# Layer 2 around a selective scan: the last sample's closing stage, halo affines, strip copies and a depthwise half rearranged

## The chip, the cores and the metric

The kernel runs on one core of one Trainium2 chip. The metric is the device time of the whole program in microseconds (us), the median of several runs.

## The reference, cut to what matters

The input is four samples of 128 channels by 128 x 128 pixels in float32. Four layers are applied to each sample, each as `x = x + layer(group_norm(x))`: a deformable convolution (layer 0), a dilated convolution in three factors (layer 1), a two-branch block with a selective scan (layer 2) and a convolution with an edge term (layer 3). The change lies in layer 2:

```python
x = cf_layernorm(x, pre_w, pre_b)          # over channels
x1, x2 = jnp.split(x, 2, axis=1)           # two halves of 64 channels
x1 = dwconv(x1, dw_w)                      # 3x3 depthwise
# ss2d(x2): in_proj -> (xx, z); xx = silu(dwconv(xx, conv_w) + conv_b)
#   forward_core: 4 directions (rows, columns, both reversed), 16 states:
#     h = h * exp(delta * A) + (delta * u) * B;   y = sum_n h * C  (+ D * u)
#   y = out_norm_w * normalised(y) + out_norm_b
#   y = y * silu(z);   out = y @ out_proj_w.T
y = interleave(x1, x2)                     # channel by channel
return cf_layernorm(y, post_w, post_b)
```

## The kernel before, in words

**Tiling.** A sample is 32 blocks of four rows, 512 pixels each (`NBLK`, `R`, `N`), with the 128 channels on the partitions. Intermediate images lie in DRAM.

**The scan.** `scan` is the main thread: 4 samples x 4 directions x 32 blocks = 512 blocks. A block has 128 channels times 16 states, held as four groups `g` of 128 x 4 x 512. For each group DVE multiplies `delta * u` (in PSUM, `dub`) with `bb` (L948) and then runs four scan instructions (L994), each of which needs a decay `pa`, an exponential made by ACT (L877, called by `decays`). One (g, ng) pair is a slot; a block has 16 slots. The outputs `h * cb` are taken on POOL (L917), summed over states on PE (L891), and copied out by `finish` (L901), which runs in slot 6 of the next block and queues the store of `y`. `prepare` makes `delta` two blocks ahead, a step per slot, on PE (`pdt` L810, `pxbc` L826), ACT (L815 to L832) and POOL (L836 to L842).

**Work beside the scan.** All other stages are generators that yield the fraction that they have done. `together` issues a slot of the scan and then pulls from the side chain `while at < f`, so the side keeps pace with the scan; `around(b)` says which stages lie beside the scan of sample b, with a weight each, and `chain` turns weights into fractions. Within a stage `weave` runs a pipeline: in round t it walks through the groups of `order`, and a step `(k, what)` handles block t-k; `MORE` advances a step that is itself a generator. There is a yield after each group. The program order on every engine is the order of issue, kept by hand (`keep_order`). Stores go through `store`, which issues them on SP a given number of ticks later; there is one tick per slot.

**layer2_pre** (L602 to L766) has 25 groups a round. It centres and normalises a block (`centre`, `square`, `spread_variance`, `invert`, `scale`), applies the affine while it writes the windows a and b of six rows (`affine`: six ACT instructions in one go, two for the block's rows and two each for the halo rows of its neighbours, L685), copies shifted rows into the windows' other halves by DMA (`shift`), and then convolves (`convolve`): six products of 128 channels for the scan's branch (`px`, L708) and six products of 64 for the depthwise half (`py`, L710), two passes each. `copy`, `gate` and `finish_strip` take the results out; every second block, `finish_strip` runs two Silus on ACT between two table loads (L740 to L742) and then, on ACT, copies the strip in column order into `cols` (L750).

**layer2_post** (L1010 to L1156) has 16 groups a round and 42 rounds. It adds up the directions (`centre`), normalises, multiplies with the gate, projects by three products (`ow_w` with the normalised y times gate, `ow_b` with the gate alone, `evc` with the depthwise half), normalises again (`square_out`, L1107 on the last two samples copies `pj` out of PSUM) and adds the skip. `measure` queues the store to `x3d`. Round n may start only when `ready(n)`: in the last direction block n-2 has been summed.

**The last sample.** Beside its scan run `layer2_post` and `layer3` of sample 2, their weights 16 and 22 times 2.5, and then its own `layer2_post` with weight 33, so that this begins 95 blocks into the 128 of the sample. What is left of it when the scan ends, and the last `layer3`, run alone.

```python
for f in main(pull):
    while at < f and pull():
        pass
    tick()
```

Of the kernel before, what the change touches and what calls it, by code (L numbers as in the profile page):

```python
# [18 lines left out]
P = 128  # L19
H = 128  # L20
# [16 lines left out]
THETA = 0.7  # L37
TW = W + 1
# [72 lines left out]
def conv_preact_kernel(ctx: ExitStack, tc: tile.TileContext, a: dict, nb: int):  # L111
# [120 lines left out]
    def image(name, parts=P):  # L232
        return dram.tile([parts, HW], F32, name=name)
# [368 lines left out]
    def layer2_pre(st):  # L602
        CH = 32
        x2d, stats = st["x2"], st["stats2"]
        zd, yd = image("zd"), image("yd", HALF)
# [3 lines left out]
        with ExitStack() as s:  # L609
# [11 lines left out]
            diag = wp.tile([P, 6, HALF], F32, name="diag")  # L621
            for t in range(6):
                nc.vector.tensor_mul(convw[:, t, :], convw[:, t, :], inx)
                nc.vector.tensor_scalar_mul(diag[:, t, :], eye2, dww[:, t : t + 1])
                yield 0.0
            sc, sh = gn_affine(stats)
# [48 lines left out]
            def affine(i):  # L675

                d = got.pop(("d", i)).rearrange("p (r w) -> p r w", w=W)
                jobs = [(i, slice(1, R + 1), slice(0, R))]
                if i > 0:
                    jobs.append((i - 1, slice(R + 1, R + 2), slice(0, 1)))  # L680
                if i + 1 < NBLK:
                    jobs.append((i + 1, slice(0, 1), slice(R - 1, R)))
                for m, to, of in jobs:
                    for t, part in zip(window(m), (slice(HALF, P), low)):
                        nc.scalar.activation(  # L685
                            t[part, to, :], d[part, of, :], AF.Identity,
                            bias=vec[part, V_PREB : V_PREB + 1], scale=vec[part, V_PREW : V_PREW + 1],
                        )

# [5 lines left out]
            def convolve(i):  # L695
                a, b = got["w", i]
                if not (stored(a) and stored(b)):
                    flush()
                got["u", i] = px = bank(0, "px")
                got["y", i] = py = bank(1, "py")  # L700
                px3 = px.rearrange("p (r w) -> p r w", w=W)
                py3 = py[low].rearrange("p (r w) -> p r w", w=W)
                use = [(1, 0, 0), (0, 0, -1), (2, 0, 1), (4, 1, 0), (3, 1, -1), (5, 1, 1)]
                for n, (t, ty, tx) in enumerate(use):
                    first, final = n == 0, n == len(use) - 1
                    co, cf = span(tx, W)
                    rf = slice(1 + ty, 1 + ty + R)
                    nc.tensor.matmul(px3[:, :, co], convw[:, t, :], a[:, rf, cf], start=first, stop=final)  # L708
                    yield
                    nc.tensor.matmul(py3[:, :, co], diag[:, t, :], b[:, rf, cf], start=first, stop=final)  # L710
                    yield

            def copy(i):
                j, q = divmod(i, BPB)
# [15 lines left out]
            def finish_strip(i):  # L730
# [8 lines left out]
                yield  # L739
                nc.scalar.activation(u, u, AF.Silu)  # L740
# [9 lines left out]
                nc.scalar.copy(got["c"][:, :, o : o + SB].rearrange("p w h -> p h w"), u)  # L750
                if (y0 + SB) % CH == 0:
                    c0 = y0 + SB - CH
                    for q in range(4):
# [8 lines left out]
                     [MORE], [(4, affine), (5, shift)], [MORE], [MORE], [(3, scale)], [MORE], [],  # L762
                     [(6, copy)], [(6, gate)], [], [(6, finish_strip), MORE], [MORE], [MORE]]
# [5 lines left out]
    def scan(pull):  # L769
# [240 lines left out]
    def layer2_post(st, engine=nc.gpsimd):  # L1010
# [6 lines left out]
        with ExitStack() as s:  # L1017
# [4 lines left out]
            event = load(wp, a["event"], [P, HALF], "event_sb")  # L1022
# [5 lines left out]
            ow_w = wp.tile([P, P], F32, name="ow_w")  # L1028
            nc.vector.tensor_scalar_mul(ow_w, po[:, 0:P], col(V_ONW))
            ow_b = wp.tile([P, P], F32, name="ow_b")  # L1030
            nc.vector.tensor_scalar_mul(ow_b, po[:, 0:P], col(V_ONB))
            pe = bank(1, "pe0")
            nc.tensor.matmul(pe[0:HALF, 0:P], event, cmat, start=True, stop=True)
            evc = wp.tile([HALF, P], F32, name="evc")
            nc.scalar.copy(evc, pe[0:HALF, 0:P])
# [19 lines left out]
            def fetch_gate(i):  # L1055
                got["z", i] = load(lp, blk(st["z"], i), [P, N], "zl", bufs=5)
                got["y", i] = load(lp, blk(st["y1"], i), [HALF, N], "yl", bufs=5)
# [33 lines left out]

            def gated(i):
                d = got["d", i]
                nc.gpsimd.tensor_mul(d, d, got["z", i])
# [45 lines left out]
            def ready(n):  # L1140
                return st["summed"] > min(max(n - 2, -1), NBLK - 1) and stored(st["y"])

            order = [[(2, r(fetch)), (3, r(fetch_gate)), (7, r(fetch_skip))], [(4, r(centre))],
                     [(5, r(spread_variance))], [(9, r(affine))], [(0, fetch_columns), (10, r(measure))],
                     [(4, r(square)), (5, r(invert))], [], [(7, r(spread_out))], [(9, r(add))], [(6, r(project))],
                     [(7, r(invert_out))], [(5, r(whiten)), (5, r(gated))], [(8, r(scale))], [], [(6, r(square_out))], []]
            if engine is nc.vector:
# [4 lines left out]
                         [(4, r(whiten))], [(5, r(square_out))], [(4, r(gated))], [(5, r(spread_out))], [],  # L1152
                         [(5, r(invert_out))]]
# [107 lines left out]
    def together(main, side):  # L1261

        at = 0.0

        def pull():
            nonlocal at
            f = next(side, 1.0)
            at = at if f is None else f
            return f is not None

        for f in main(pull):
            while at < f and pull():
                pass
            tick()
        drain(side)
# [4 lines left out]
    def loads(engine, stage, spare=False):  # L1280
# [3 lines left out]
        beside.clear()  # L1284
# [19 lines left out]
    def around(b):  # L1304
# [11 lines left out]
def layouts(i):  # L1316
# [54 lines left out]
    x["event"] = c((np.repeat(np.eye(HALF, dtype=f), 2, axis=1) * (np.arange(P) % 2 == 0).astype(f)).T)  # L1371
# [25 lines left out]
```

## Time and profile before

| what | us |
|---|---|
| median of three runs | 22394.33 (22386.31 to 22396.27) |
| profiled execution, its own time | 22863.03 |
| its span | 22861.3 |
| before the scan | 0 to 2552 |
| the scan | 2552 to 22532 |
| `layer2_pre` (samples 0 to 3) | 2291 to 3280, 6379 to 7766, 11873 to 13074, 17171 to 18372 |
| `layer2_post` (samples 0 to 3) | 7766 to 8331, 13074 to 13639, 18372 to 19596, 21249 to 22587 |
| `layer3` of the last sample, alone | 22587 to 22861 |

The profile is one execution with every instruction recorded; it is 2.1% longer than the median of the runs. In its lines a group reads: source line, engine, operation, output <- inputs, shapes, count, then busy time and mean ns of one, then the engine's idle time just before such instructions and what ended most of that. PE is TensorE, PEld its weight loads, DVE VectorE, ACT ScalarE, POOL GpSimd, SP the queue that issues DMAs. A table of stretches has the stretch, its length, then busy time with (x instructions) for each engine, or for the chosen line alone, and last the granted TensorE clock, the share of time that the DMA engines were busy, and GB/s. A line of waits has engine, line, what it waited for, and the total in us, the number of times and the longest. A timeline line has start, duration, engine, line, operation, tiles and in brackets the idle time before it with what ended that.

### The profile page before, as it was taken

What the parts mean: (1) busy time and instruction counts of PE and PEld (TensorE: products, weight loads), DVE (VectorE), ACT (ScalarE), POOL (GpSimd) and SP (SyncE); (2) the same over time, 40 slices, a digit from 0 to 9 for tenths busy, and PEclk for the clock granted to TensorE, in tenths of its full rate; (3) what the DMA queues carried; (4) which work ended last, traced back from release to release, by engine and by line L of the source; (5) the groups of instructions that cost most, each with busy time, mean ns of one, the idle gap of its engine ahead of it and who ended that gap; (6) DMA issues with size and microseconds to landing.
All of it is one profiled execution on the core that took longest, in us unless ns stands there. A gap on an engine that the chain in (4) does not pass through costs nothing. (4 is left out here: it accounts for less than half of the span.)

```text
span 22861.3 us, 179349 instructions
## 1 busy us (share of the span) xinstructions
PE 16937.6 (74%) x38024; PEld 6604.5 (29%) x38024; DVE 18834.7 (82%) x19765; ACT 16444.8 (72%) x37282; POOL 17193.3 (75%) x11496
## 2 busy tenths in 40 slices
PE   3445886666878888766689888766688978778768
PEld 1112222222323333222233333322232323233223
DVE  3443489999998899888898899988898899999863
ACT  4665677888778766788868776688877867666553
POOL 3554477787788888777788788877778889877763
PEclk7667898888989999887799999977899999999989
DMA  7556468777756777777776687777776677555653
GB/s 216 176 173 186 149 204 289 246 244 238 249 202 211 220 237 258 240 245 235 239 246 206 208 252 243 248 239 243 245 254 203 209 222 220 190 195 201 195 171 112
DMA packets 2560083, 5005.34 MB, mean 219 GB/s; under 512 B 1059136, under 2 KB 1330952, under 8 KB 2416656
## 3 DMA queue, kind: packets, MB, share of 16 engines
q1 hardware_dynamic: 2190352, 3785.61, 51.1%
q0 software_dynamic: 368640, 1208.25, 17.5%
q8 instruction: 310, 5.08, 0.1%
q14 instruction: 781, 6.40, 0.1%
HBM read 4065.12 MB, written 857.74 MB: 215 GB/s over the span
## 5 line engine op out<-in xcount | busy, mean ns | idle before, releaser
L994 DVE TENSOR_TENSOR_SCAN h<-pa,carry,h 128x512 f32<-128x512 f32 x8192 | 9999.6, 1268 | 977.3 <-ACT pa L877 764.5
L917 POOL TENSOR_TENSOR h<-h,cb 128x1024 f32<-128x1024 f32 x3740 | 8779.6, 2360 | 1429.8 <-ACT carry L911 1416.5
L891 PE MATMUL yacc<-h,gather_sb 128*128 128x512 f32 x15264 | 8345.2, 676 | 1600.5 <-POOL h L917 1106.9
L421 POOL DMA_INDIRECT g<-table,idx x4608 | 4542.8, 986 | 2073.0 <-issue 1273.7
L877 ACT ACTIVATE pa<-spread,neg_a 128x512 f32<-128x512 f32 x8192 | 5482.6, 682 | 279.2 <-DVE h L994 232.4
L948 DVE TENSOR_TENSOR h<-dub,bb 128x2048 f32<-128x2048 f32 x2048 | 4664.7, 2278 | 626.2 <-ACT dub L857 386.5
L891 PEld LDWEIGHTS yacc<-h,gather_sb 128*128 128x128 f32 x15264 | 3117.0, 216 | 5970.8 <-issue 3375.1
L458 PE MATMUL pst<-ident,v 128*128 128x128 f32 x4608 | 1190.9, 371 | 3038.5 <-DVE v L450 1719.6
L911 ACT COPY carry<-h 128x2 f32<-128x2 f32 x4096 | 769.4, 188 | 3089.9 <-DVE h L994 3084.6
L435 ACT ACTIVATE g<-g,wt 128x128 f32<-128x128 f32 x9216 | 2851.9, 389 | 113.6 <-DMA g<-table,idx 64.3
L447 DVE TENSOR_TENSOR pw<-pw,g 128x512 f32<-128x512 f32 x2304 | 1599.2, 694 | 1439.1 <-ACT pw L435 1180.3
L435 ACT ACTIVATE pw<-g,wt 128x128 f32<-128x128 f32 x4608 | 1695.6, 368 | 760.4 <-remote 278.2
L458 PEld LDWEIGHTS pst<-ident,v 128*128 128x128 f32 x4608 | 718.5, 159 | 4394.0 <-issue 2406.8
L836 POOL TENSOR_TENSOR e<-e,one_e 128x512 f32<-128x512 f32 x512 | 650.2, 1270 | 1372.0 <-ACT one_e L830 1304.3
L468 PE MATMUL acc<-smp,w_sb 128*128 128x512 f32 x2304 | 1558.3, 765 | 77.3 <-DVE x L475 68.9
L857 ACT COPY dub<-spread 128x512 f32<-128x512 f32 x2048 | 1199.3, 586 | 421.4 <-DVE h L948 241.9
L450 DVE SCALAR_TENSOR_TENSOR v<-g,wt,pw 128x128 f32<-128x128 f32 x4608 | 1293.3, 343 | 114.0 <-DVE pw L447 1.8
L1212 PE MATMUL p<-xn,w_l_sb 128*128 128x508 f32 (+2 forms) x2304 | 1138.6, 612 | 1.8 <-ACT xn L1191 1.8
L708 PE MATMUL px<-win,convw_sb 128*128 128x508 f32 (+1 forms) x1536 | 838.8, 628 | 4.7 <-DMA win<-win 4.7
L710 PE MATMUL py<-win,diag 128*64 128x508 f32 (+1 forms) x1536 | 832.7, 624 | 0.0
L826 PE MATMUL pxbc<-u,xbc_sb 128*128 128x512 f32 x1024 | 583.6, 653 | 330.5 <-DVE h L948 318.3
L462 ACT COPY smp<-pst 128x512 f32<-128x512 f32 x1152 | 664.6, 577 | 202.3 <-remote 163.6
(172 smaller groups left out, 16990.0 us busy)
## 6 DMA issues: line engine op xcount, KB each, us to landing
spread<-stepsd SPq DMA_DIRECT2D x2048, 512.0 KB
bb<-bcd SPq DMA_DIRECT2D x512, 1024.0 KB
cb<-bcd SPq DMA_DIRECT2D x512, 1024.0 KB
stepsd<-steps SPq DMA_DIRECT2D x512, 512.0 KB
table<-gt SPq DMA_DIRECT2D x512, 256.0 KB
g<-table,idx POOLq DMA_INDIRECT x4608
u<-urow SPq DMA_DIRECT2D x256, 256.0 KB
yrow<-y SPq DMA_DIRECT2D x256, 256.0 KB
```

The source lines that it names most:

```text
L421: nc.gpsimd.indirect_dma_start(out=g[:, r].rearrange("p q c -> p (q c)"), out_offset=None, in_=table, in_offset=bass.IndirectOffsetOnAxis( ...
L435: nc.scalar.activation(pw[:, r * P : (r + 1) * P] if c == 0 else g[:, r, c, :], g[:, r, c, :], AF.Copy, scale=wv[:, r, q, k, c : c + 1],)
L447: nc.vector.tensor_add(pw, pw, g[:, :, c, :])
L450: nc.vector.scalar_tensor_tensor(v[:, r, :], g[:, r, 3, :], wv[:, r, q, k, 3:4], pw[:, r, :], ALU.mult, ALU.add)
L458: nc.tensor.transpose(pst[:, r * P : (r + 1) * P], v[:, r, :], ident)
L468: nc.tensor.matmul(got["a", i], w0[:, k, :], got.pop(("c", n)), start=k == 0, stop=k == KK - 1)
L857: nc.scalar.copy(p, blocks[t]["p", g][:, 1, :])
L877: nc.scalar.activation(pa, blocks[t]["p", g][:, 0, :], AF.Exp, scale=neg_a[:, k, n : n + 1])
L891: nc.tensor.matmul(c["y"], gather[:, g, :], c["h", g][:, ng, :], start=g == 0 and ng == 0, stop=last and ng == parts[-1] and not second,)
L917: engine.tensor_mul(h, h, c["cb"][:, 2 * half : 2 * half + 2, :])
L948: nc.vector.tensor_tensor(h, c["pdu", g].unsqueeze(1).to_broadcast([P, NG, N]), c["bb"], ALU.mult)
L994: nc.vector.tensor_tensor_scan(o, f, o, carry[:, n : n + 1], ALU.mult, ALU.add)
```

## The change

1. The last sample. The side chain's unit for the last sample becomes 138 blocks rather than 128 (`LATE` = 10), and `together` scales the scan's fraction by `share` to match. The stages of sample 2 get 96 units, the last `layer2_post` 42, one for each of its 42 rounds: round n goes beside block 96+n of the sample, and ten rounds come after the scan. Samples 0 to 2 keep their pace.
2. `affine` becomes three steps of two ACT instructions each, in groups 13, 15 and 18 of the round; `shift` goes from group 13 to group 17.
3. In `finish_strip` the scan's next decay is issued ahead of the Silus (`beside["decays"]`), and the copy into `cols` goes from ACT to DVE. `beside` is no longer cleared as a whole.
4. The depthwise half: taps 0 to 2 and 3 to 5 are put side by side in one `diag` of 128 columns, so that three products give two partial results, the upper 64 rows one image row below. Both are stored (`yd` has 128 rows, the upper half written one row earlier and its last row zeroed), and `layer2_post` adds them by an `event` matrix stacked twice.
5. In `layer2_post` the norm's weight and bias are applied by an ACT step (`colour`) and the product with `ow_b` is dropped; `whiten`, `colour` and `gated` get new places in both orders.

```diff
-            diag = wp.tile([P, 6, HALF], F32, name="diag")
+            diag = wp.tile([P, 3, P], F32, name="diag")
             for t in range(6):
                 nc.vector.tensor_mul(convw[:, t, :], convw[:, t, :], inx)
-                nc.vector.tensor_scalar_mul(diag[:, t, :], eye2, dww[:, t : t + 1])
+                half = slice(t // 3 * HALF, (t // 3 + 1) * HALF)
+                nc.vector.tensor_scalar_mul(diag[:, t % 3, half], eye2, dww[:, t : t + 1])
                 yield 0.0
+            nc.sync.dma_start(yd[HALF:P, (H - 1) * W :], zero[HALF:P, 0:W])
...
-            def affine(i):
...
+            def affine(to_block):
+
+                to = {0: slice(1, R + 1), -1: slice(R + 1, R + 2), 1: slice(0, 1)}[to_block]
+                of = {0: slice(0, R), -1: slice(0, 1), 1: slice(R - 1, R)}[to_block]
+
+                def one(i):
+                    d = got["d", i].rearrange("p (r w) -> p r w", w=W)
+                    if not 0 <= i + to_block < NBLK:
+                        return
+                    for t, part in zip(window(i + to_block), (slice(HALF, P), low)):
                         nc.scalar.activation(
                             t[part, to, :], d[part, of, :], AF.Identity,
...
-                    nc.tensor.matmul(py3[:, :, co], diag[:, t, :], b[:, rf, cf], start=first, stop=final)
-                    yield
+                    if ty == 0:
+                        nc.tensor.matmul(py3[:, :, co], diag[:, t, :], b[:, rf, cf], start=first, stop=n == 2)
+                        yield
...
-                yt = pp.tile([HALF, N], F32, name="yt")
-                nc.scalar.copy(yt, got.pop(("y", i))[low])
-                store(blk(yd, i), yt)
+                yt = pp.tile([P, N], F32, name="yt")
+                nc.scalar.copy(yt, got.pop(("y", i)))
+                store(blk(yd, i)[low], yt[low])
+                out = W if i == 0 else 0
+                store(yd[HALF:P, i * N - W + out : (i + 1) * N - W], yt[HALF:P, out:])
...
+                if "decays" in beside:
+                    beside["decays"]()
                 nc.scalar.activation(u, u, AF.Silu)
                 nc.scalar.activation(z, z, AF.Silu)
...
-                nc.scalar.copy(got["c"][:, :, o : o + SB].rearrange("p w h -> p h w"), u)
+                nc.vector.tensor_copy(got["c"][:, :, o : o + SB].rearrange("p w h -> p h w"), u)
...
-                     [MORE], [(4, affine), (5, shift)], [MORE], [MORE], [(3, scale)], [MORE], [],
-                     [(6, copy)], [(6, gate)], [], [(6, finish_strip), MORE], [MORE], [MORE]]
+                     [MORE], [(4, affine(-1))], [MORE], [(4, affine(0)), MORE], [(3, scale)], [(5, shift)],
+                     [(4, affine(1)), MORE], [(6, copy)], [(6, gate)], [], [(6, finish_strip), MORE], [MORE], [MORE]]
...
         def decays(at):
 
+            beside["decays"] = lambda: decays(at + 1)
...
+            def colour(i):
+                d = got["d", i]
+                nc.scalar.activation(d, d, AF.Identity, bias=col(V_ONB), scale=col(V_ONW))
...
-                nc.tensor.matmul(pj, ow_w, got.pop(("d", i)), start=True, stop=False)
-                nc.tensor.matmul(pj, ow_b, got.pop(("z", i)), start=False, stop=False)
+                nc.tensor.matmul(pj, owc, got.pop(("d", i)), start=True, stop=False)
                 nc.tensor.matmul(pj, evc, got.pop(("y", i)), start=False, stop=True)
...
-            order = [[(2, r(fetch)), (3, r(fetch_gate)), (7, r(fetch_skip))], [(4, r(centre))],
+            order = [[(2, r(fetch)), (3, r(fetch_gate)), (7, r(fetch_skip))], [(4, r(centre)), (6, r(gated))],
...
-                     [(4, r(square)), (5, r(invert))], [], [(7, r(spread_out))], [(9, r(add))], [(6, r(project))],
-                     [(7, r(invert_out))], [(5, r(whiten)), (5, r(gated))], [(8, r(scale))], [], [(6, r(square_out))], []]
+                     [(4, r(square)), (5, r(invert))], [], [(7, r(spread_out))], [(5, r(whiten)), (9, r(add))],
+                     [(6, r(project))], [(7, r(invert_out))], [(5, r(colour))], [(8, r(scale))], [],
+                     [(6, r(square_out))], []]
...
-    def together(main, side):
+    def together(main, side, share):
...
-            while at < f and pull():
+            while at < f * share and pull():
...
-        return [(stage, 2.5 * w) for stage, w in side] + [(loads(None, layer2_post(sts[b]), True), 33)]
-
-    together(scan, chain([(chain(around(b)), 1) for b in range(nb)]))
+        load, rounds = sum(w for _, w in side), NBLK + 10
+        side = [(stage, (NDIR * NBLK + LATE - rounds) * w / load) for stage, w in side]
+        return side + [(loads(None, layer2_post(sts[b]), True), rounds)]
+
+    over = 1 + LATE / (NDIR * NBLK)
+    side = chain([(chain(around(b)), over if b == last else 1) for b in range(nb)])
+    together(scan, side, nb / (nb - 1 + over))
```

More of the change, by code (lines that the diff above doesn't have):

```diff
@@ L37 @@
 THETA = 0.7
+LATE = 10
 TW = W + 1
@@ L604, in layer2_pre @@
         x2d, stats = st["x2"], st["stats2"]
-        zd, yd = image("zd"), image("yd", HALF)
+        zd, yd = image("zd"), image("yd")
         urow, ucol = image("urow"), image("ucol")
@@ L673, in window @@
                 return got["w", i]
-            def affine(i):
[L677 to L684, printed above, removed]
+            def affine(to_block):
[6 more added lines that the diff above has]
+                    for t, part in zip(window(i + to_block), (slice(HALF, P), low)):
                         nc.scalar.activation(
@@ L688, in affine @@
                         )
+                return one
             def shift(i):
@@ L701, in convolve @@
                 px3 = px.rearrange("p (r w) -> p r w", w=W)
-                py3 = py[low].rearrange("p (r w) -> p r w", w=W)
+                py3 = py.rearrange("p (r w) -> p r w", w=W)
                 use = [(1, 0, 0), (0, 0, -1), (2, 0, 1), (4, 1, 0), (3, 1, -1), (5, 1, 1)]
@@ L1021, in layer2_post @@
             outt = load(wp, a["outt"], [P, P], "outt_sb")
-            event = load(wp, a["event"], [P, HALF], "event_sb")
+            event = load(wp, a["event"], [P, P], "event_sb")
             cmd = wp.tile([P, P], F32, name="cmd")
@@ L1027, in layer2_post @@
             nc.tensor.matmul(po[:, 0:P], outt, cmat, start=True, stop=True)
[L1028 to L1031, printed above, removed]
+            owc = wp.tile([P, P], F32, name="owc")
+            nc.scalar.copy(owc, po[:, 0:P])
             pe = bank(1, "pe0")
-            nc.tensor.matmul(pe[0:HALF, 0:P], event, cmat, start=True, stop=True)
-            evc = wp.tile([HALF, P], F32, name="evc")
-            nc.scalar.copy(evc, pe[0:HALF, 0:P])
+            nc.tensor.matmul(pe[:, 0:P], event, cmat, start=True, stop=True)
+            evc = wp.tile([P, P], F32, name="evc")
+            nc.scalar.copy(evc, pe[:, 0:P])
             got = {}
@@ L1056, in fetch_gate @@
                 got["z", i] = load(lp, blk(st["z"], i), [P, N], "zl", bufs=5)
-                got["y", i] = load(lp, blk(st["y1"], i), [HALF, N], "yl", bufs=5)
+                got["y", i] = load(lp, blk(st["y1"], i), [P, N], "yl", bufs=5)
             def fetch_skip(i):
@@ L1090, in whiten @@
                 engine.tensor_mul(got["d", i], got.pop(("p", i)), got.pop(("s", i)))
+            def colour(i):
+                d = got["d", i]
+                nc.scalar.activation(d, d, AF.Identity, bias=col(V_ONB), scale=col(V_ONW))
             def gated(i):
                 d = got["d", i]
-                nc.gpsimd.tensor_mul(d, d, got["z", i])
+                nc.gpsimd.tensor_mul(d, d, got.pop(("z", i)))
             def project(i):
                 got["q", i] = pj = bank(2, "pj3")
-                nc.tensor.matmul(pj, ow_w, got.pop(("d", i)), start=True, stop=False)
-                nc.tensor.matmul(pj, ow_b, got.pop(("z", i)), start=False, stop=False)
+                nc.tensor.matmul(pj, owc, got.pop(("d", i)), start=True, stop=False)
                 nc.tensor.matmul(pj, evc, got.pop(("y", i)), start=False, stop=True)
@@ L1151, in layer2_post @@
                          [], [(4, r(spread_variance))], [], [(4, r(invert)), (6, r(add))], [(5, r(project))], [],
-                         [(4, r(whiten))], [(5, r(square_out))], [(4, r(gated))], [(5, r(spread_out))], [],
-                         [(5, r(invert_out))]]
+                         [(4, r(whiten))], [(5, r(square_out))], [(4, r(colour))], [(5, r(spread_out))],
+                         [(4, r(gated))], [(5, r(invert_out))]]
             yield from weave(NBLK, order, ready)
@@ L1283, in loads @@
             yield f
-        beside.clear()
+        beside["busy"], beside["spare"] = None, False
     def head(b):
@@ L1370, in layouts @@
         x["gather"][:, g, g * Q : (g + 1) * Q] = np.repeat(np.eye(Q, dtype=f), P // Q, axis=0)
-    x["event"] = c((np.repeat(np.eye(HALF, dtype=f), 2, axis=1) * (np.arange(P) % 2 == 0).astype(f)).T)
+    x["event"] = c(np.tile((np.repeat(np.eye(HALF, dtype=f), 2, axis=1) * (np.arange(P) % 2 == 0).astype(f)).T, (1, 2)))
     x["eye2"] = np.tile(np.eye(HALF, dtype=f), (2, 1))
```

## Prediction

> **What bounds the kernel now.** The page first, for what is busiest; then the scan's own line by stretch, because the busy shares average over stages.
>
> ```profile
> PE 16937.6 (74%) x38024; PEld 6604.5 (29%) x38024; DVE 18834.7 (82%) x19765; ACT 16444.8 (72%) x37282; POOL 17193.3 (75%) x11496
> L994 DVE TENSOR_TENSOR_SCAN h<-pa,carry,h 128x512 f32<-128x512 f32 x8192 | 9999.6, 1268 | 977.3 <-ACT pa L877 764.5
> ```
>
> The scan (L994, 16 to a block) sits on DVE, and what DVE waits for is mostly the exponential `pa` from ACT. Next, five stretches with L994 alone: length, busy, (scans).
>
> ```profile
> 11900.00:13050.00 1150.00, 675.97 (x558) 0.96 0.64 208
> 18370.30:19378.70 1008.40, 618.31 (x512) 0.93 0.75 222
> 19857.90:21281.50 1423.60, 925.72 (x769) 0.96 0.57 197
> 21281.50:21867.50 586.00, 309.77 (x257) 0.89 0.65 191
> 21867.50:22531.60 664.10, 310.87 (x256) 0.85 0.56 166
> ```
>
> Length times 16 over scans is the block time: 33.0 us beside `layer2_pre` (sample 2's window; samples 1 and 3 are alike), 31.5 beside sample 2's `layer2_post`, 29.6 beside `layer3` (near DVE's floor: four products of 2.28 and sixteen scans of 1.2 are 28.3), then 36.5 and 41.5 beside the last `layer2_post`. The same stage thus costs 31.5 once and 39.0 on average the second time. The waits of 21281 to 22531 (total, times, longest) and one block's timeline say why.
>
> ```profile
> DVE h L994 <- ACT pa L877: 301.6, 29, 13.9
> ```
> ```profile
> ACT d L1107 <- DMA x3d<-d: 193.0, 22, 10.8
> ```
> ```profile
> 22059.57 0.33 SPq L126 DMA_DIRECT2D yrl<-yrow  x1
> ...
> 22062.53 4.01 SPq L148 DMA_DIRECT2D x3d<-d  x1
> ...
> 22069.07 0.58 ACT L1107 COPY d<-pj 128x512 f32<-128x512 f32 x1 [10.35 <-DMA x3d<-d]
> ...
> 22070.86 1.28 DVE L994 TENSOR_TENSOR_SCAN h<-pa,carry,h 128x512 f32<-128x512 f32 x1 [13.45 <-ACT pa L877]
> ```
>
> 42 rounds were to fit 33 blocks, but round n may not start before block n-2 is summed. So each falls behind and is issued whole in one slot, just after `finish`. Its loads need the y stored a moment before; the old x3d store queues behind them on SP; ACT's L1107 needs that store's buffer; the next `pa` is behind L1107. One stall of 13 us per block.
>
> In `layer2_pre` ACT stops the scan too (same kind of view, 12227 to 12252):
>
> ```profile
> 12227.53 3.65 ACT L685 ACTIVATE win<-d,vec_sb 64x512 f32<-64x512 f32 x6
> ...
> 12231.79 4.81 DVE L994 TENSOR_TENSOR_SCAN h<-pa,carry,h 128x512 f32<-128x512 f32 x4 [0.57 <-ACT pa L877]
> ...
> 12246.21 1.28 DVE L994 TENSOR_TENSOR_SCAN h<-pa,carry,h 128x512 f32<-128x512 f32 x1 [4.33 <-ACT pa L877]
> 12246.63 1.91 ACT L750 COPY cols<-u 128x1024 f32<-128x1024 f32 x1
> ...
> 12249.68 1.28 DVE L994 TENSOR_TENSOR_SCAN h<-pa,carry,h 128x512 f32<-128x512 f32 x1 [2.19 <-ACT pa L877]
> ```
>
> Six affines in a row, and two Silus between two table loads, then the strip's copy: each makes `pa` late. Sorting the 110.5 us that L994 waits for `pa` in 11900 to 13050 by what ACT ran just before gives: Silus 55, strip copy 10, affines 38, the rest 7.
>
> **The Trainium skill.** ScalarE: Activation LUTs, "What ACT_TABLE_LOAD costs": about 1283 ns and a drain; the trace has 1283 for each load, two per strip, and shows no drain. SBUF — State Buffer, "Door 1": SBUF has 16-byte lines, and an access that leaves its line pays; the trace agrees: the strip copy (L750), which writes with a 128-byte step, takes 1.96 us, the Silu of as many elements 1.06. Same page, "two separate sides": DVE and GpSimd share one port pair as an exclusive lock, taken by a two-port copy; the trace agrees: the 144-element cast L317 takes 0.235 us at the median, 3.876 at most.
>
> **The change, part by part** (profile time).
>
> *Equal shares.* Round n now goes with block 96+n, one of its 16 groups after each slot. The y that it loads was stored about seven slots earlier, the x3d store goes out seven slots before L1107, so the 13 us stall has no cause. Nearest row: 31.5 a block. 32 blocks: 1250.1 (586.0+664.1) - 1008 = **-242**. Ends: 29.6 a block (-302), 33.6 a block (-175), what the blocks at 18998 and 19032 took (33.7 and 33.3), where a round began within a slot of its block. What is late next: POOL, with eight products of 2.36 and eight small ones of 1.27 (four of `prepare`, four of the round), 29.0 per block. After the scan ten rounds are left, not nine: 55.4/9 = **+6**. The colour step (ACT, 0.81 like L1124) hides under 70% busy ACT.
>
> *Depthwise in three.* Three products fewer per block, each of two passes (L710, x2 in the timeline 1.07 us, the next one 1.0 us after it). Before the scan, `layer2_pre` of sample 0 is bound by PE (101.5 us busy of 110 in 2330 to 2440): ten convolved blocks x 3 x 1.0 = **-30** (ends -32, -15 if ACT takes over). Beside the scan PE isn't what DVE waits for; but ACT waits about 31 us a stage for PE (`e` 10.6, `y` 6.6, `yt` 5.7, `pv` 4.9, `z` 3.6 in 11900 to 13050), and some of that reaches `pa`: **-20** for four stages (ends -40, 0). The wider `yt` takes ACT the same time; its second store and the doubled load add 128 KB each per block to SP's queue, about 0.5 us of issue, with SP ahead of the compute.
>
> *Halo in three steps.* L685's halo form takes 0.49 us and its block form 0.81, two of each: 0.98, 1.62 and 0.98 us in place of 3.65; DVE has one to two `pa` in hand, so most of the 38 us a stage goes. Over four stages the affine's share was 34+35+38+38 = 145; I take three quarters: **-108** (ends -145, -50). The copies between halves of the window (`shift`) go out four groups later, 2.9 slots or 6 us. The trace's margin from issue to first use is 16 us at the median, 4 at the least: cover enough, a few blocks excepted. If it were gone, PE would stand at `convolve`, with the scan's sums queued behind it.
>
> *Strip: one more `pa` ahead, copy on DVE.* The extra `pa` is worth one scan, 1.2 us. But the copy (DVE is in order) waits for the first Silu, which ends 2.4 us after the table load starts, 3.05 with the extra exponential ahead of it; the scans are queued behind. The copy's own time isn't in the trace: 0.7 as a contiguous two-port copy (an estimate from VectorE: DVE Perf Modes, "The perf-mode tier table", 1.227 us for 2048 elements), 4.4 if it pays for its step and waits out a POOL product (2.0+2.36). I take 2.0, ACT's time with its step. I went through the strips in the scan (59) with each one's own order: where the copy falls in the Silus' slot (about half, `pa` returning 7.2 us after the table load) the mean is -0.2, else +0.7. So 0.25 us gained on each: **-15** (ends: 1.3 gained, -75; 2.1 lost, +124).
>
> *Sample 0 to 2's `layer2_post`.* One pair of passes less, one ACT step of 0.81 more, 128 KB more per round where DMA is already at 0.91: **0** (ends -25, +35). The rest (`beside` cleared key by key, the wider constants, one zero row) is set-up beside other work: 0.
>
> Sum: -242 +6 -30 -20 -108 -15 = **-409**. From the profiled execution's 22863.0 that is 22454; the median of the runs is 22394.3, 2.1% less, so I scale: -401, **21993**.
>
> **Rivals.**
> - *Nothing comes late* (chance 0.15): 29.6 a block and a 0.7 us copy: -302+6-30-30-130-75 = -561, scaled 21845. For it: the blocks either side of sample 2's bad ones take 29.84. Against: POOL's 29.0 leaves nothing.
> - *The bad phase is kept for good* (0.17): every round begins at slot 0, where POOL's small products crowd slots 7 to 12 and `pdt` waits behind late sums. For it: blocks at 19065 and 19102 took 36.7 and 37.1 with the round's `centre` ahead of `pdt`. Against: now `centre` comes after `pdt`, and `gated` moved to slot 1, away from the crowd. 32 x 36.9 = 1181, so -69 in place of -242: -236, 22163. If the shares did nothing at all, near 22230.
> - *The strip copy holds the scan* (0.12): 4.4 us each, +124: -270, 22130.
> - *Windows late, slower than before* (0.06): if the later halves take over about 10 us to land, PE stands in `convolve` in each of the 118 blocks beside the scan. It decides from 409/118 = 3.5 us of DVE per block; at 5 us, +590-409 = +181, 22571. Against: the 16 us margin.
>
> The forecast has 0.50. About 0.2% (45 us) is what a measurement of this kernel can tell from no change. Of the last rival's 0.06, 0.05 is slower by more than that and 0.01 within; another 0.01 within is left to the others; faster is 0.93. The range, 21840 to 22200, takes in the first three rivals.
>
> **What would show it.** Right: blocks 96 to 127 of sample 3 at 30 to 33 us, no ACT wait for x3d, `pa` waits in `layer2_pre` down from 110 to about 60 us, each with a DVE copy of about 2 us near a Silu; the stretch before the scan 30 us shorter; ten rounds in the tail. Wrong: last blocks at 36 or more with DVE waiting for `dub`; strip copies of 4 us; PE waiting for `win`.

## The result, and the profile after

The changed kernel takes **22011.65 us** (median, 21994.19 to 22014.76), beside 22395.3 us (22386.31 to 22400.01) for the kernel before on the same chip: ratio 0.9828, 95% interval 0.9811 to 0.9845, or 384 us less. The prediction was 21993, range 21840 to 22200.

One thing has to be known to read the profiles side by side. The profile of before that the prediction used, 22863.03 us, is not long because it was recorded. Below, the kernel before has medians of 22819 to 22847 us on two other chips, with or without a profile, and of 22382 to 22395 on the chips where the changed kernel was measured; on which chip the first profile was taken isn't on record. Nearly all of the difference lies ahead of the scan: the first convolution (L708 before, L714 after) starts at 2335.3 us in the first profile and at 1912.2 in the one after. So stages are compared below by their lengths, and totals by their ratio to the kernel before on the same chip.

The page's line of busy times and the scan's line (L994 has become L1006), after:

```profile
PE 16320.8 (74%) x37000; PEld 6656.8 (30%) x37000; DVE 18917.1 (86%) x19821; ACT 16414.8 (75%) x37350; POOL 17221.0 (78%) x11496
L1006 DVE TENSOR_TENSOR_SCAN h<-pa,carry,h 128x512 f32<-128x512 f32 x8192 | 9996.2, 1267 | 486.5 <-ACT pa L889 274.1
```

The scan's instructions cost what they did; the idle time just before them has halved (977.3 to 486.5), and the part put down to `pa` has gone from 764.5 to 274.1. The stretches with L1006 alone, after (stretch, length, busy, scans, granted clock, DMA share, GB/s), are: beside `layer2_pre` of sample 2; beside `layer2_post` of sample 2; the first and second half of the last 32 blocks; the closing rounds after the scan.

```profile
11380.00:12510.00 1130.00, 674.11 (x556) 0.90 0.66 215
17752.40:18710.00 957.60, 593.21 (x491) 0.93 0.74 226
20686.20:21181.00 494.80, 311.98 (x259) 0.93 0.74 228
21181.00:21677.00 496.00, 308.17 (x254) 0.93 0.74 226
21677.00:21738.50 61.50, 0.08 (x1) 0.92 0.35 122
```

Length times 16 over scans: 32.5 us a block beside `layer2_pre` (33.0 before), 31.2 beside sample 2's `layer2_post` (31.5), and 30.6 and 31.2 in the last blocks (36.5 and 41.5 before). The last 32 blocks take 990.8 us instead of 1250.1. What DVE waited for there (total, times, longest):

```profile
DVE h L1006 <- ACT pa L889: 31.6, 27, 1.5
...
DVE h L960 <- ACT dub L869: 12.4, 25, 0.5
DVE h L960 <- POOL h L929: 10.7, 23, 0.7
```

The wait of 13.9 us at worst has become one of 1.5 us, and ACT has no wait for `x3d` left. Beside `layer2_pre` the picture is different. DVE's waits in blocks 91 to 127 of sample 1 (sample 2's `layer2_pre`; 36 blocks), first before (from the second profile of before, `e0_before_again` below), then after:

```profile
DVE h L994 <- ACT pa L877: 110.7, 57, 5.5
DVE h L948 <- ACT dub L857: 17.2, 37, 3.9
DVE h L948 <- issue: 15.0, 19, 2.0
```
```profile
DVE h L1006 <- ACT pa L889: 39.7, 39, 2.4
DVE cols L761 <- ACT u L751: 30.9, 13, 5.6
DVE h L960 <- issue: 18.3, 23, 7.6
DVE h L960 <- ACT dub L869: 18.0, 34, 3.6
```

The scan's own waits fell by 71 us, but 31 us came back one line up, as DVE standing before the strip copy.

By stage, from the scan's starts in the first profile of before and in the one after: first convolution to first scan 216.4 to 187.4 (-29); the 136 blocks beside `layer2_pre` (0 to 20 and 85 to 127 of sample 0, 92 to 127 of samples 1 and 2) 4500 to 4450 (-50); the last 32 blocks -259; the closing rounds 55.4 to 61.5 (+6); the blocks beside the other three `layer2_post` -18. That is -350, where the runs on one chip say -374 to -384. The other stretches of the scan, beside the early layers and `layer3`, are 75 us shorter in the profile after. About half of that goes with the chip: the changed kernel and its variants take 11748 to 11762 us there on the chips where the kernel before is short, and 11792 to 11796 on the others. Two profiles of before differ by 27 us there between themselves, so nothing is read from these stretches.

### The profile page after: what moved, and what is told of

It is laid out like the page before. It is cut to its first block, busy times and chain, and to the rows that moved or that the text cites. A ratio compares the mean times of both kernels' runs of the same rounds, so it can differ in the third digit from the quotient of the medians.

```text
span 22013.0 us, 177442 instructions
## 1 busy us (share of the span) xinstructions
PE 16320.8 (74%) x37000; PEld 6656.8 (30%) x37000; DVE 18917.1 (86%) x19821; ACT 16414.8 (75%) x37350; POOL 17221.0 (78%) x11496
## 5 line engine op out<-in xcount | busy, mean ns | idle before, releaser
L1006 DVE TENSOR_TENSOR_SCAN h<-pa,carry,h 128x512 f32<-128x512 f32 x8192 | 9996.2, 1267 | 486.5 <-ACT pa L889 274.1
L714 PE MATMUL px<-win,convw_sb 128*128 128x508 f32 (+1 forms) x1536 | 792.4, 614 | 34.8 <-DMA win<-win 34.8
L931 POOL TENSOR_TENSOR h<-h 128x512 f32<-128x512 f32 x558 | 711.5, 1275 | 43.7
L822 PE MATMUL pdt<-u,wd 128*128 128x512 f32 x1024 | 555.0, 624 | 204.8 <-DVE h L960 155.3
```

What stands on the lines that cost most here:

```text
L1006: nc.vector.tensor_tensor_scan(o, f, o, carry[:, n : n + 1], ALU.mult, ALU.add)
```

## The experiments

Runs of one group share a chip and the runs of before there. A kernel that ran on another chip than the changed one is compared with it by the ratios.

**Is it the profile or the chip?** `e0_before_again` is the kernel before, unchanged.

> The kernel before, unchanged, for a second profile: the first profiled execution took 22863 us where the runs take 22395, and the stretch before the scan (0 to 2552) was 452 us longer than in the changed kernel, in code that the change leaves alone. Theory A (that execution was an odd one): its time is near 22395, layer 0 ahead of the scan takes about 1490 us as in the changed kernel, and the last 32 blocks still take 1250 us. Theory B (profiling slows this kernel, and slows most where DMA waits are exposed): again near 22860, and the last 32 blocks take less than 1250 us when not profiled.

Measured: 22844.07 us under the profile, and 22847.01 (median, 22833.95 to 22872.34) in the nine runs of before on this chip. The time is what theory B said, but not for its reason: the profile costs nothing, and 22395 against 22847 goes with the chip. The variants of the changed kernel show where it lies: with the same code ahead of the scan, `e3` and `e4` reach the first convolution at 2337 and 2344 us on this chip, `e5` to `e8` at 1913 to 1920 on another. The page's line for layer 0's gathers, before in this run, and after:

```profile
L421 POOL DMA_INDIRECT g<-table,idx x4608 | 4565.8, 991 | 2048.0 <-issue 1240.1
```
```profile
L422 POOL DMA_INDIRECT g<-table,idx x4608 | 4559.7, 990 | 1635.0 <-issue 1061.2
```

The same gathers, 991 and 990 ns each, with 413 us less idle time ahead of them in the second. No part of the change touches them, and `e3`, which is the changed kernel but for the strip copy and ran on e0's chip, has 2058.4 us ahead of them. What makes these gaps longer isn't settled.

**The shares alone.** `e1_shares_alone` is before with `LATE`, `share` and the new weights of `around`.

```diff
-            while at < f and pull():
+            while at < f * share and pull():
...
-        return [(stage, 2.5 * w) for stage, w in side] + [(loads(None, layer2_post(sts[b]), True), 33)]
+        load, rounds = sum(w for _, w in side), NBLK + 10
+        side = [(stage, (NDIR * NBLK + LATE - rounds) * w / load) for stage, w in side]
+        return side + [(loads(None, layer2_post(sts[b]), True), rounds)]
```

> The kernel before with the equal shares for the last sample alone (LATE, the weights, share). Theory A: nearly all that the last stage gave comes from here: 32 blocks at 31 us in place of 39, ten rounds in the tail: 22395 - 253 = 22142. Theory B (the steps' new order in layer2_post, with colour apart, is what brought the blocks to 31 us): the blocks stay at about 33.5 us as in sample 2's blocks with the round's start at the block's start, 22395 - 178 + 6 = 22223.

Measured: 22672.71 us against 22847.01, ratio 0.9921 (0.9906 to 0.9936), 174 us less, which is theory B's amount. The last 32 blocks in two halves, then their waits on DVE and two on ACT:

```profile
21263.30:21776.70 513.40, 309.49 (x256) 0.90 0.71 215
21776.70:22322.30 545.60, 310.70 (x256) 0.92 0.67 202
```
```profile
DVE h L949 <- issue: 63.5, 25, 3.5
ACT e L816 <- POOL h L918: 37.0, 12, 3.1
DVE h L995 <- ACT pa L878: 36.2, 26, 3.9
...
ACT e L816 <- PE pdt L811: 29.7, 11, 4.0
```

32.1 and 34.1 us a block: the 13 us stall is gone, but the shares alone miss 31.5. DVE now stands before its product (L949). The profile names nothing that it waits for, but in 19 of the 25 times `dub` was ready only 0.09 us before the product, behind an `e` for which ACT had stood. ACT's two waits for `e` shown here come to 67 us, and to 4 in the changed kernel.

**The shares with the new `layer2_post`.** `e11_shares_and_new_post` adds to e1 the changed places, the colour step and the two products, with the depthwise half as before.

```diff
-                     [(4, r(square)), (5, r(invert))], [], [(7, r(spread_out))], [(9, r(add))], [(6, r(project))],
-                     [(7, r(invert_out))], [(5, r(whiten)), (5, r(gated))], [(8, r(scale))], [], [(6, r(square_out))], []]
+                     [(4, r(square)), (5, r(invert))], [], [(7, r(spread_out))], [(5, r(whiten)), (9, r(add))],
+                     [(6, r(project))], [(7, r(invert_out))], [(5, r(colour))], [(8, r(scale))], [],
+                     [(6, r(square_out))], []]
```

> The kernel before with the equal shares and with the changed layer2_post's order, colour step and two products, but with the depthwise half, the halo and the strips as before. Theory A, the new places of gated and whiten give what the shares alone lacked: the last 32 blocks take about 990 us (1059 with the shares alone, 1267 before), and the whole is about 245 us below before, ratio 0.989. Theory B, the rest came with the other edits (narrower work on PE, other phases of the buffers): the last 32 blocks stay at about 1050 us, ratio 0.992.

Measured: 22566.84 us against 22819.14, ratio 0.989 (0.9875 to 0.9905), 252 us less: theory A. The last 32 blocks and DVE's waits:

```profile
21224.90:21719.80 494.90, 309.52 (x257) 0.94 0.74 222
21719.80:22222.90 503.10, 310.66 (x256) 0.93 0.74 220
```
```profile
DVE h L995 <- ACT pa L878: 31.5, 26, 1.5
...
DVE h L949 <- issue: 15.8, 13, 2.8
```

998 us, within 7 of the changed kernel. L949's unnamed wait fell from 63.5 to 15.8. So the -259 of the last stage is made of two parts that the prediction priced as one: the pace, and the new `layer2_post`. Whether in the latter the places, the colour step on ACT or the dropped product count for most wasn't tried.

**The depthwise half alone.** `e10_depthwise_alone` is before with the three products, the wider `yd`, stores, loads and constants.

```diff
-                    nc.tensor.matmul(py3[:, :, co], diag[:, t, :], b[:, rf, cf], start=first, stop=final)
-                    yield
+                    if ty == 0:
+                        nc.tensor.matmul(py3[:, :, co], diag[:, t, :], b[:, rf, cf], start=first, stop=n == 2)
+                        yield
```

> The kernel before with the depthwise half in three products alone (with its wider stores, loads and constants). Theory A, the prediction's steps: the stretch before the scan 30 us shorter, and 20 us more over the four layer2_pre beside the scan: ratio about 0.9978. Theory B, PE's three products are paid only where PE sets the pace: 30 us before the scan and nothing beside it, or a loss of up to 10 us per stage from the 128 KB more per block in each direction: ratio 0.9987 or above.

Measured: 22767.04 us against 22819.14, ratio 0.9979 (0.9972 to 0.9985), 52 us less, in sum what the step said (-50), but split otherwise: 19 us ahead of the scan and 26 to 30 in the blocks beside `layer2_pre` (4474 us, 4500 and 4505 in the two profiles of before). From the first convolution to the first scan, before and in e10 (length, then busy time of PE, PEld, DVE, ACT and POOL, granted clock, DMA share, GB/s):

```profile
2322.90:2538.70 215.80, 164.80 (x309) 42.22 (x308) 2.29 (x1) 123.81 (x177) 22.93 (x19) 0.90 0.33 95
```
```profile
2326.40:2523.30 196.90, 126.93 (x250) 50.80 (x248) 2.29 (x1) 120.50 (x177) 22.88 (x19) 0.81 0.38 111
```

PE loses 38 us of work, the stretch only 19. PE's share falls from 76% to 64%, with a granted clock of 0.81 instead of 0.90, and ACT's is 61%: no engine fills the stretch any more. In its place PE stands longer for ACT: its wait for `z` to be copied out, ahead of the next block's `pd`, grew from 6.1 to 21.5 us. That is the prediction's lower end, "-15 if ACT takes over".

**The halo alone.** `e13_halo_alone` is before with the affine in three steps and the later `shift`.

```diff
-                     [MORE], [(4, affine), (5, shift)], [MORE], [MORE], [(3, scale)], [MORE], [],
-                     [(6, copy)], [(6, gate)], [], [(6, finish_strip), MORE], [MORE], [MORE]]
+                     [MORE], [(4, affine(-1))], [MORE], [(4, affine(0)), MORE], [(3, scale)], [(5, shift)],
+                     [(4, affine(1)), MORE], [(6, copy)], [(6, gate)], [], [(6, finish_strip), MORE], [MORE], [MORE]]
```

> The kernel before with the affine in three steps and the later shift alone; strips, depthwise half and shares as before. Theory A, the prediction's step, which was masked in the changed kernel because the strip copy's wait for the Silu took the room: here about 108 us are gained (50 to 145), ratio 0.995 (0.9935 to 0.998). Theory B, the steps behind two affines still make the exponential late, and the few us a stage that are saved are taken by the next wait (DVE for the inputs, ACT behind the Silus) whatever the strips do: 0 to 30 us, ratio 0.9987 or above, with the waits behind affines falling from 38 to between 20 and 30 us in a stage.

Measured: 22852.12 us against 22845.73, ratio 1.0 (0.9992 to 1.0009). Nothing, where the prediction put 108 us: theory B. In the blocks beside `layer2_pre` its profile is rather longer, 4520 us for 4500 and 4505. The waits of the same 36 blocks, beside the 110.7, 17.2 and 15.0 of before shown above:

```profile
DVE h L996 <- ACT pa L879: 104.8, 63, 5.5
DVE h L950 <- issue: 25.6, 19, 7.9
DVE h L950 <- ACT dub L859: 19.9, 37, 4.1
```

Sorted by what ACT ran just before, the scan's waits behind affines did fall in this stage, from 38 to 23 us; those behind other ACT work rose from 7 to 15, and DVE's waits ahead of its product, all causes together, by 15. One of these, 7.9 us, comes from a window that is late: PE stands for it.

```profile
PE px L710 <- DMA win<-win: 6.2, 1, 6.2
```

The changed kernel has it too, in the same block of samples 2 and 3. Its timeline in sample 3 shows the chain that the fourth rival described:

```profile
17320.03 2.04 PE L714 MATMUL px<-win,convw_sb 128*128 128x512 f32 x2 [7.14 <-DMA win<-win]
...
17331.36 1.02 PE L822 MATMUL pdt<-u,wd 128*128 128x512 f32 x2
...
17332.48 0.69 ACT L827 ACTIVATE e<-pdt,vec_sb 128x512 f32<-128x512 f32 x1 [9.96 <-PE pdt L822]
...
17333.77 0.59 ACT L869 COPY dub<-spread 128x512 f32<-128x512 f32 x1
...
17334.45 2.29 DVE L960 TENSOR_TENSOR h<-dub,bb 128x2048 f32<-128x2048 f32 x1 [10.41 <-issue]
```

7.1 us late at PE, `pdt` queued behind the convolution, `dub` behind `e` on ACT: 10.4 us at DVE, which the profile calls "issue". `e6` below keeps the later `shift` and has no wait of 5 us or more there, so it is not the shift alone that makes the window late.

**The halo in one step again.** `e6_halo_in_one` is the changed kernel with the three affine steps in one group, `shift` left in its new place.

```diff
-                     [MORE], [(4, affine(-1))], [MORE], [(4, affine(0)), MORE], [(3, scale)], [(5, shift)],
-                     [(4, affine(1)), MORE], [(6, copy)], [(6, gate)], [], [(6, finish_strip), MORE], [MORE], [MORE]]
+                     [MORE], [(4, affine(0)), (4, affine(-1)), (4, affine(1))], [MORE], [MORE], [(3, scale)], [(5, shift)],
+                     [MORE], [(6, copy)], [(6, gate)], [], [(6, finish_strip), MORE], [MORE], [MORE]]
```

> The changed kernel with the affine's six instructions in one group again (group 13), the rest as changed. Theory A (the halo burst cost 38 us a stage and splitting it took most of that): +25 us a stage, about +90 over the four stages against the changed kernel on this chip. Theory B (the time that the split saved went into the wait of the strip copy and into other waits, because ACT has as much to do as before): under +30.

Measured: 22013.44 us against 22382.43, ratio 0.9837 (0.9823 to 0.985), 5 us above the changed kernel beside it (e5, below): not told apart from it. Its waits:

```profile
DVE h L1006 <- ACT pa L889: 51.0, 39, 3.5
DVE cols L761 <- ACT u L751: 28.7, 13, 4.8
...
DVE h L960 <- issue: 12.8, 20, 4.4
```

11 us more for `pa`, 6 us less of "issue" and 2 us less at the strip. Theory B again: from both sides, what the halo's split buys is too small to be measured.

**The strip.** Three kernels change the strip alone. `e3_copy_on_act` puts the copy back on ACT:

```diff
-                nc.vector.tensor_copy(got["c"][:, :, o : o + SB].rearrange("p w h -> p h w"), u)
+                nc.scalar.copy(got["c"][:, :, o : o + SB].rearrange("p w h -> p h w"), u)
```

> The changed kernel with the strip copy back on ACT, the decay ahead of the Silus kept. Theory A: on DVE the copy stands in front of the scans until the Silu is done (262 us of waiting for 57 strips) and takes 1.2 to 2.9 us; on ACT it delays the next decay by 2 us instead; the two weigh about the same, 21985 (21950 to 22040). Theory B: ACT is what the scan waits for, so the move to DVE was a gain, and undoing it costs the copy's 1.96 us on 59 strips: 22012 + 116 = 22128.

`e7_no_decay_ahead` drops the extra decay ahead of the Silus:

```diff
-                if "decays" in beside:
-                    beside["decays"]()
                 nc.scalar.activation(u, u, AF.Silu)
```

> The changed kernel without the extra decay ahead of the Silus, the copy still on DVE. Theory A (the extra decay lets DVE run one scan longer, 1.2 us on 59 strips, but only where the copy doesn't already hold it; after the copy the decay was ready in time): +0.5 to 1 us a strip, +30 to +60. Theory B (the copy alone sets the wait, which the extra decay makes 0.67 longer): -40 to 0.

`e4_copy_two_slots_later` keeps the copy on DVE but lets the scan issue it, behind the second scan that follows:

```diff
+                def columns():
...
+                if "decays" in beside and i < NBLK - 1:
+                    beside["columns"] = [2, columns]
...
                     nc.vector.tensor_tensor_scan(o, f, o, carry[:, n : n + 1], ALU.mult, ALU.add)
+                    if beside.get("columns"):
+                        beside["columns"][0] -= 1
+                        if beside["columns"][0] == 0:
+                            beside.pop("columns")[1]()
```

> The changed kernel with the strip copy still on DVE, but issued two scans later, where DVE would stand waiting for the next decay anyway. Theory A: the wait for the Silu in front of the scans goes (31 us a stage) and the copy's 1.2 us lies in the wait for the decay: about 1.5 us a strip for 59 strips, 21925 (21890 to 21970). Theory B: ACT's 4.7 us between the table loads has to be waited out in any case, and the wait only goes from the copy back to the decay: 22012 (21995 to 22030).

Measured, each against before on its chip: e3 22491.04, ratio 0.9841 (0.9828 to 0.9855); e7 22001.63, ratio 0.9826 (0.9813 to 0.984); e4 22411.98, ratio 0.9808 (0.9794 to 0.9821). The changed kernel, in `e5_after_again`:

> The changed kernel, unchanged, beside the others on one chip. The kernel before took 22394 us on one chip and 22847 on another, and the difference lies ahead of the scan. Theory A: the change's effect doesn't depend on that; the scan (first to last scan instruction) lasts 19576 us again, 0.983 of the time before, or 390 us less where before takes 22850 (22460). Theory B: the first chip's ratio was also better by 0.2%, 22500.

it took 22007.95 against 22382.43, ratio 0.9834 (0.9821 to 0.9847). So moving the copy to DVE is worth 0.07%, some 16 us, which the intervals don't separate from nothing; the extra decay is worth nothing (-6 us without it, inside the spread); and moving the copy two scans later is worth 0.26%, some 58 us more: theory A for e3 and e4, theory B for e7. The gain of e4 compares two chips, and the intervals overlap in part; but on one chip `e4` takes 79 us less than `e3`, and the blocks beside `layer2_pre`, where the strips lie, take 4379 us in `e4`, 4446 in `e3` and 4435 to 4450 in the changed kernel and in `e7`. `e5` landed on a chip where the kernel before is short, so whether the change is worth the same on the others wasn't tried. The copy itself, on DVE in the changed kernel and on ACT in e3 (ns: least, median, most):

```profile
L761 DVE COPY cols<-u x64: 1018/1164/2890, 1940.4 to 17781.5; 128x1024 f32<-128x1024 f32 x64
...
  ACT u L751: 262.0, 57
```
```profile
L761 ACT COPY cols<-u x64: 1904/1963/2015, 2368.1 to 18259.2; 128x1024 f32<-128x1024 f32 x64
```

The copy itself is cheap; what it waits for costs more. Of the 262 us, 133 belong to four strips ahead of the scan, where DVE has little else to do; within the scan it is 129 us in 53 strips, 2.4 us each. The longest, after:

```profile
11657.43 0.69 ACT L889 ACTIVATE pa<-spread,neg_a 128x512 f32<-128x512 f32 x1
...
11659.78 0.69 ACT L889 ACTIVATE pa<-spread,neg_a 128x512 f32<-128x512 f32 x1
...
11660.48 1.28 ACT L751 ACT_TABLE_LOAD   x1
...
11661.77 1.06 ACT L751 ACTIVATE u<-u 128x1024 f32<-128x1024 f32 x1
...
11662.86 1.71 DVE L761 COPY cols<-u 128x1024 f32<-128x1024 f32 x1 [5.57 <-ACT u L751]
...
11664.42 1.25 DVE L1006 TENSOR_TENSOR_SCAN h<-pa,carry,h 128x512 f32<-128x512 f32 x1
```

Two exponentials are ready, at 11658.1 and 11660.5, while DVE stands before the copy until 11662.9 and both scans behind it. In e4 these two scans run first, and the wait before the copy in the same 36 blocks shrinks from 30.9 us to 2.6, while the scan's own grows from 39.7 to 51.6:

```profile
DVE h L1014 <- ACT pa L897: 51.6, 48, 3.0
...
DVE cols L762 <- ACT u L751: 2.6, 3, 1.0
```

**Where in the block a round begins.** Two kernels take e4 and move the last rounds by half and by three quarters of a block.

```diff
-LATE = 10
+LATE = 10.5
```

> The changed kernel with the copy two slots later (as in the earlier run) and the last sample's rounds half a block later (LATE 10.5), so that a round's 16 groups run from slot 8 to slot 7. The copy: 35 us less than the changed kernel, as in that run's scan time. The half block, theory A (POOL's small products of the round crowd those of prepare in slots 7 to 12; half a block apart they don't): the last 32 blocks go from 31.0 to 30.0 us, -32, tail +3. Theory B (POOL is full, 29.0 of 31 us, so the place doesn't matter): 31.0 as before, or worse if the round's centre now comes ahead of pdt as in sample 2's worst blocks (up to 37, +190).

Measured: 21933.97 us against 22382.43, ratio 0.9801 (0.9788 to 0.9815). The last 32 blocks took 970 us (988 to 991 in e3 to e7), 21 less, where theory A said 32.

```diff
-LATE = 10
+LATE = 10.75
```

> The changed kernel with the strip copy two scans later, and the last sample's rounds begun three quarters of a block after the scan's block (LATE = 10.75) in place of at its start. Theory A, any start away from slot 0 keeps the round's group 0 and its small products out of the slots where prepare's crowd POOL and ACT: last 32 blocks about 970 us as with the start at half a block, ratio 0.980. Theory B, only half a block away is right, since at three quarters the round's later groups fall on slots 4 to 8 where prepare and finish stand: about 990 us, ratio 0.981.

Measured: 22342.52 us against 22819.14, ratio **0.9793** (0.978 to 0.9806), 477 us less than before. The last 32 blocks and their waits for `pa`:

```profile
21035.40:21509.60 474.20, 307.98 (x257) 0.95 0.76 234
21509.60:21984.60 475.00, 308.37 (x256) 0.97 0.78 238
```
```profile
DVE h L1014 <- ACT pa L897: 2.2, 1, 2.2
```

29.5 and 29.7 us a block, what blocks beside `layer3` take, and better than either theory said. In the changed kernel a round's group 5 (`square`, `invert`: four ACT instructions) falls behind slot 5, where ACT also has `prepare`'s and, soon after, `finish`'s work: the scan of slot 7 waited 1.2 us in 26 of the 32 blocks, nearly all of the 31.6 us. Three quarters of a block later that wait is gone. e12 is the fastest kernel here: its ratio is 0.4% below the changed kernel's, which was measured on another chip, and e8 was 74 us faster than the changed kernel on the same one.

## Why the prediction was right, point by point

The total was right (384 us for 401), and the largest term was right in cause. The halo term was wrong, and that the sum came out only 17 us off is in part luck. The four `layer2_pre` stages beside the scan gained 50 us where the steps had 143 (20, 108 and 15). The last stage and its tail gave 17 more than said and the other `layer2_post` 18. What is left, 24 to 34 us, lies in stretches that the prediction put at nothing and that no profile here can price.

- **Equal shares, -242: right in mechanism, slightly low.** The stall was the round issued whole; with a group after each slot it went (e1), and ACT's wait for `x3d` with it. But 31.5 a block wasn't the shares' doing alone: e1 stayed at 33.1, near the upper end of the range, and the remaining 61 us came with the rearranged `layer2_post` (e11), which the step mentioned only as cover (the colour step "hides"). "What is late next: POOL" held for e1 only in part: part of ACT's wait for `e` was for a POOL product (37.0 us), and `e` made `dub` late. Whole: -259.
- **Ten rounds after the scan, +6:** 55.4 to 61.5, as said.
- **Depthwise, -30 and -20:** -52 together (e10), of which 19 ahead of the scan. The step priced ten blocks at three products of 1.0 us each; PE's work did fall by 38 us, but then PE stood 15 us longer for ACT. With the other edits it came to -29, the last part with the strip copy off ACT: the stretch took 192.9 us with the copy back on ACT (e3), 186 to 190 with it on DVE.
- **Halo, -108: wrong.** It measured 0 alone (e13) and 5 us when undone (e6). The step that failed is "DVE has one to two `pa` in hand, so most of the 38 us a stage goes". Splitting the burst moves ACT's work, it doesn't remove any. In the stage looked at, the scan's waits behind affines fell by 15 us, not by the 27 that three quarters of the burst's share come to; the affines now stand before `dub` and other `pa`, and the waits there rose by 23. Part of that is one block, in this stage and in sample 3's, in which a late window cost 5 to 10 us.
- **Strip, -15: too small to be told.** Some 16 us for the copy and nothing for the extra decay fit the step, but the runs can't tell either from nothing. The DVE copy took 1.16 us at the median, not 2.0, and the wait for the Silu was the cost, as the step said. The extra decay, held to be worth 1.2 us a strip, was worth nothing measurable.
- **`layer2_post` of samples 0 to 2, 0:** -18, less than two profiles of before differ by elsewhere, and inside the step's lower end (-25).
- **The scaling of 409 to 401** rested on the profile being longer than the runs. It was the chip; unscaled the sum would have been 8 us further off.
- **The rivals.** "Nothing comes late" took place only with e12's other phase. The bad phase wasn't kept. The strip copy did hold the scan, by 2.4 us on average and 5.6 at most, but as a wait that replaced the earlier `pa` wait, not on top of it. "Windows late" took place in single blocks, with just the chain described.

What stays open: shares with `layer2_post` (-252), depthwise (-52) and halo (0), each alone, add up to about 300 us, and the strip copy's 16 makes 316, against 374 measured in e5. The intervals of the single runs (15 to 35 us each) can hold most of that gap, but the profiles show where some of it lies: beside `layer2_pre`, the depthwise half alone takes 26 to 30 us less than before (e10) and the halo alone 15 to 19 more (e13), while e3, which has both and the extra decay, takes 54 to 59 less. Whether depthwise and halo help each other or the extra decay does it while the copy is on ACT wasn't tried.

## What to carry to other kernels

Spread a background pipeline over the slots of the thread that it feeds from, then try its phase: here three quarters of a block took 41 us off the last 32 blocks after everything else was done (e4 to e12). An instruction put on an engine that runs in order costs the wait for its input besides its own time; place it behind work that is ready (here two scans, some 58 us). Cutting a burst into pieces gains only what the pieces then don't delay: list what each piece stands in front of before crediting the burst's whole stall.

## What the runs showed of the hardware

- The same program, the kernel before, differs by 424 to 465 us (2%) between chips. Nearly all of it lies ahead of the scan, in a stretch of indirect gathers: in the changed kernel and its variants the first convolution starts at 2319 to 2344 us in e3, e4 and e12 and at 1912 to 1920 in the others, with the gathers' own duration unchanged (992 ns in e3, 990 after). What makes the gaps longer isn't settled; a profiled execution should be compared with runs on its own chip before anything is called the cost of profiling.
- A DVE copy of 128 x 1024 float32 with a 128-byte step in its output took 1.02 to 1.10 us in the 31 strips of the changed kernel's profile that began with no POOL product under way. The other 33 ended 0.89 to 0.94 us after the POOL product that was under way, and so took up to 2.89: the copy stood until that product was done. The prediction's upper end had this wait; the median of 1.16 hides it.
- The same copy took ACT 1.96 us, where its Silu of as many elements takes 1.06. The Trainium skill, SBUF — State Buffer, "Door 1", has an access that leaves its 16-byte line pay, and ACT's time agrees with that. Whether DVE pays isn't shown: no contiguous copy of that size ran there.
- With fewer products in a stretch the granted TensorE clock was lower (0.90 to 0.81, e10, with PE busy for 64% of the stretch instead of 76%). The products that stayed took no longer for it: the 120 of `px` came to 68 us before and 65 in e10.
